# The first steps of a masked attention layer begin with one mask quarter and half of the heads; the other mask pieces and projections are made beside the steps

## The chip, the cores and the metric

The kernel runs on one core of a Trainium2 chip. Its time is device microseconds (us) of one execution, and the number that stands for a kernel is the median of several runs. Five engines work side by side: PE (TensorE, matrix products and transposes), DVE (VectorE), ACT (ScalarE), POOL (GpSimd) and SP (SyncE, which here only issues transfers). PEld is PE's loading of weights. Each engine runs its own queue in order and waits on semaphores for the others.

## The reference, cut to what matters

```python
# x: (8, 2048, 256) f32;  adj: (2048, 2048) int32, about 0.8% ones, symmetric, diagonal set
qkv = einsum('fnc,ck->fnk', x, w_qkv)             # H = 8 heads of D = 32
scores = einsum('fnhd,fmhd->fhnm', q, k) / sqrt(D)
scores = where(adj > 0, scores, -1e9)             # one mask for all entries and heads
t = einsum('fhnm,fmhd->fnhd', softmax(scores), v)
x1 = layernorm(x + t) * ln1_g + ln1_b
h = relu(x1 @ w1 + b1)
x2 = layernorm(x1 + h @ w2 + b2) * ln2_g + ln2_b
out = layernorm(x + x2)
```

## The kernel before

**Steps.** The main loop goes over `items`: 8 batch entries f, 4 quarters qc of 512 query rows, 2 groups g of 4 heads, 16 blocks mb of 128 keys. That is 1024 steps, 128 to an entry and 16 to a group. One step t does, in this order:

- `advance(t)`: some side work (below);
- `exponentials(items[t + 1])`: ACT, 128x2048, in place (L237);
- `scores(items[t + 2])` (`LEAD` is 2): PE makes the scores of four heads, transposed, keys in partitions (8 matmul records a step, L230), into two of three PSUM pairs; DVE adds the mask and writes the `p` tile, two instructions of 128x1024 (L233);
- `values(items[t])`: PE multiplies by the values (L249);
- `add_up(items[t])`: the sums over blocks. Of 16 blocks, six are added by POOL (L271) and six by transfers that POOL issues and that add in memory (L268); the block's tile is free after that. Four tiles (blocks 0, 1, 2 and 14) stay until the group's `denominator` has multiplied them by ones on PE (L315).

`p` tiles come from the pool `pp` with 12 buffers.

**The mask.** DVE adds it as float8: 0 where `adj` is set, -57344 elsewhere (int8 -5 has the same bits). A quarter has 8 pieces of 128x2x512 bytes, in the pool `mkp` of 9 buffers. All pieces also lie in device memory (`MD`), and `load_mask` (L151, on SP) fetches the next quarter's pieces in the second half of each quarter, one every second step, from step 17 of 32 on: 13 steps ahead of their first use.

**Side work.** Turned inputs (`turn`), queries (`ask`), keys and values (`project`) of the next entry, denominators, the division, the feed-forward part and the norms are generators in `fill`, sorted by a due step. `advance` gives PE a credit of 2200 a step; one product over 512 columns (in four column parts) costs 2048. A generator that yields `BANK` wants one of the PSUM banks for side work: at most one is started in a step, and only with a credit of 1024 or more left or something overdue; one that yields `MORE` holds its bank and goes on, in the next step if the credit is gone.

**The start.** `begin()` (L550 to L597) runs before step 0 and works through 16 chunks of `adj`, 512x512 each, quarter by quarter, fetched a little ahead into `p` tiles. For each, DVE compares the integers with 0 (L575, two instructions, bf16 out), PE turns the blocks (L141, 16 transposes), ACT casts one half to int8 (L147) and DVE takes the minimum with 1 into float8 for the other (L145); SP stores both in `MD`. With the chunks of quarter 0 go the turned inputs of entry 0, its first queries, and keys and values of the first head group (g = 0); with those of quarter 1, keys and values of g = 1. The scores of steps 0 and 1 come after quarter 1, and then the chunks of quarters 2 and 3.

Of the kernel before, what the change touches and what calls it, by code (L numbers as in the profile page):

```python
# [29 lines left out]
BANK, MORE, WAIT, TURNED, ROOM, INPUTS = -1, -2, -3, -4, -5, -10  # L30
STEP, UNIT, TURN, KEPT = 2200, 1024, 1400, 2200

MASKED = -57344.0
CODE = -5.0


# [25 lines left out]
def fast_path(ctx, tc, cst, x, adj, out, RS):  # L62
# [52 lines left out]
    def take(shape, dt):  # L115
        live.pop(0)
        live.append(ld.tile(shape, dt, name="in"))
        return live[-1]

    def give(t):  # L120
        live[:] = [None if u is t else u for u in live]


    MD = dp.tile([NCK, MB // 2, P, 2 * CH // 4], I32, name="md")
    MK = {}

    def words(mask):
        return mask.rearrange("p b q -> p (b q)").bitcast(I32)

    def mask_piece(t, qc, k):  # L130
        MK[t, qc, k] = mkp.tile([P, 2, CH], F8, name="mask")
        return MK[t, qc, k]

    def mask_blocks(qc, mc, cv, to=None):
        for half in range(2):
            yield BANK
            ps = bank(BF16)
            for r in range(2):
                for j in range(TPC):
                    rr = 2 * half + r  # L140
                    nc.tensor.transpose(ps[:, r, j * P:(j + 1) * P], cv[:, j, rr * P:(rr + 1) * P], identb)  # L141
            k = 2 * mc + half
            m = to[half] if to else mask_piece(0, qc, k)
            if half:
                nc.vector.tensor_tensor(m, ps, cst["ones"][:, 0:1, None].to_broadcast([P, 2, CH]), ALU.min, saturate=False)  # L145
            else:
                nc.scalar.copy(m.bitcast(I8), ps)  # L147
            nc.sync.dma_start(MD[qc, k], words(m))

    def load_mask(f, qc, k):  # L150
        nc.sync.dma_start(words(mask_piece(f, qc, k)), MD[qc, k])  # L151
# [5 lines left out]
    def queries(f, c, xT):  # L157
        for g in range(2):
            yield from channels(QT, qp, "qT", (f, c, g), xT, g * P)

    def turn_rows(xc, xT):
        for a in range(2):
            yield BANK
            ps = bank()
            transposes(ps, [xc[:, j, a * P:(a + 1) * P] for j in range(TPC)])
            nc.scalar.copy(xT[:, a, :], ps)
# [367 lines left out]
                resume(e, t)  # L534

    items = [(f, qc, g, mb) for f in range(F) for qc in range(NCK) for g in range(2) for mb in range(MB)]
    LEAD = 2
    FRAME = 2 * NCK * MB


# [7 lines left out]
            104: [(project, 0, 1)], 108: [(project, 1, 1)], 112: [(project, 2, 1)], 116: [(project, 3, 1)]}  # L548

    def begin():  # L550
        todo = deque((qc, c) for qc in range(NCK) for c in range(NCK))
        rows, cols = [], deque()

        def fetch():
            if todo:
                qc, c = todo.popleft()
                t = pp.tile([P, 4, CH], F32, name="p").bitcast(I32)
                nc.sync.dma_start(t, adj[qc * CH:(qc + 1) * CH, c * CH:(c + 1) * CH].rearrange("(j p) m -> p j m", p=P))
                cols.append((qc, c, t))

        for c in range(NCK):
            rows.append(pp.tile([P, 4, CH], F32, name="p"))
            xc = rows[c][:, 0:2, :].rearrange("p a (b c) -> p (a b) c", c=C)
            nc.sync.dma_start(xc, x[0, c * CH:(c + 1) * CH, :].rearrange("(j p) c -> p j c", p=P))
            fetch()
        fetch()
        while cols:
            qc, c, col = cols.popleft()
            if c % 2 == 0:
                two = pp.tile([P, 4, CH], F32, name="p").rearrange("p a q -> p (a q)").bitcast(BF16)  # L570
            cv = two[:, c % 2 * TPC * CH:(c % 2 + 1) * TPC * CH].rearrange("p (j m) -> p j m", m=CH)

            for half, what in enumerate((CODE, MASKED)):
                part = slice(half * 2 * P, (half + 1) * 2 * P)
                nc.vector.tensor_scalar(cv[:, :, part], col[:, :, part], 0.0, what, op0=ALU.is_le, op1=ALU.mult)  # L575
            fetch()
            xT = rows[c][:, 2:4, :]
            if qc == 0:
                yield from turn_rows(rows[c][:, 0:2, :].rearrange("p a (b c) -> p (a b) c", c=C), xT)
                nc.sync.dma_start(XD[0][c], xT)  # L580
                XT[0, c] = xT
                if c == 0:
                    yield from queries(0, 0, xT)
                yield from project(0, c, 0, xT)
            elif qc == 1:
                yield from project(0, c, 1, xT)
            if qc and c % 2 == 0:
                out4 = take([P, 4, 2, CH], F8)
                give(out4)
            yield from mask_blocks(qc, c, cv, [out4[:, c % 2 * 2 + i] for i in range(2)] if qc else None)  # L590
            if (qc, c) == (1, NCK - 1):
                for k in range(LEAD):
                    scores(items[k])
                exponentials(items[0])

    for _ in begin():
        pass  # L597
    state["side"] = 0
    for t, (f, qc, g, mb) in enumerate(items):
        if g == 1 and mb % 2 and (f + 1 < F or qc + 1 < NCK):  # L600
            load_mask(f + (qc + 1) // NCK, (qc + 1) % NCK, mb // 2)
        for what, *which in NEXT.get(t % FRAME, []):
            to = f if what is ask and which[0] else f + 1
            if to < F:
# [266 lines left out]
```

## Time and profile before

| | us |
|---|---|
| median of 5 runs | 3243.46 (3241.08 to 3250.44) |
| profiled execution, its own time | 3251.11 |
| its span, first to last instruction | 3249.2 |
| PE busy | 3114.1 (96%) |
| DVE busy | 2736.7 (84%) |
| ACT busy | 2437.0 (75%) |
| POOL busy | 2592.1 (80%) |
| first scores (L230) begin | 60.62 |
| third scores begin (the loop) | 98.34 |
| DMA engines, transfers that add (`p<-p`) | 66.9% of 16 engines' span |

How to read it: a line of the profile names the line of the code, the engine, the operation and `out<-in` by the program's tile names. In the timeline the first two numbers are the start and the length in us, and the bracket gives how long the engine idled before and what ended that. The granted clock (PEclk) is the share of full speed that TensorE was given. Busy time of PE holds pipelined matmuls, so 96% is not 96% of its peak. A queue name ending in q, as SPq, is an engine's issuing of a transfer; the time to landing is counted from there.

### The profile page before, as it was taken

To read this page: it belongs to the slowest core of one execution; us is meant where nothing else is said; L and a number is where in the kernel's file an instruction comes from. 1 tells how busy PE (TensorE), PEld (TensorE's weight loads), DVE (VectorE), ACT (ScalarE), POOL (GpSimd) and SP (SyncE) were. 2 spreads that over 40 slices of the span, in tenths; PEclk is the share of its full clock that TensorE was granted. 3 is DMA by queue.
4 is the path that set the end of the run, shared out by engine and by line. 5 is a ranking of instruction groups with operands and counts; after the bars stand their busy time and mean duration, and the time that the engine had idled before them with its cause. 6 is when DMAs were issued, how large, how long until landed. Compare 5 with 4: busy or idle time off the path is not lost.

```text
span 3249.2 us, 68406 instructions
## 1 busy us (share of the span) xinstructions
PE 3114.1 (96%) x28996; PEld 980.6 (30%) x28996; DVE 2736.7 (84%) x3203; ACT 2437.0 (75%) x1941; POOL 2592.1 (80%) x1358
## 2 busy tenths in 40 slices
PE   7899999999999999999999999999999999998985
PEld 4222333223332233322333323323233323332222
DVE  4788888888888888888988888888888888888975
ACT  3667778778777777778777778777778777777764
POOL 0578888888888888788887888888888788878884
PEclk8899999999999999999999999999999999999998
DMA  9688789778879788789788879878789778877763
GB/s 317 144 184 180 184 179 196 177 180 192 183 176 206 170 189 195 158 194 201 178 180 174 181 175 220 176 168 197 173 194 199 175 171 199 180 171 161 166 143 86
DMA packets 153240, 590.52 MB, mean 182 GB/s; under 512 B 15040, under 2 KB 67776, under 8 KB 103904
## 3 DMA queue, kind: packets, MB, share of 16 engines
q0 software_dynamic: 64416, 434.80, 66.9%
q1 hardware_dynamic: 87696, 149.98, 13.1%
q8 instruction: 229, 3.75, 0.4%
q10 hardware_dynamic: 816, 1.31, 0.1%
q14 instruction: 83, 0.68, 0.1%
HBM read 146.67 MB, written 37.75 MB: 57 GB/s over the span
## 4 chain that ended last, share of the span: by engine, by line
PE 75%; DVE 7%; POOL 5%; DMA 4%; issue 4%; ACT 2%; DVEq 0%; ACTq 0%; POOLq 0%
PE s L230 28%; PE x L249 24%; PE x L54 14%; PE x L315 6%; DVE p L233 5%; PE x L95 4%; DMA p<-p 3%; POOL p L271 2%; ACT p L237 1%; DMA mask<-md 1%; POOL y L365 1%; POOL y L363 0%; DVE st L278 0%; DMA y<-in_x_dram 0%; POOL y L461 0%
## 5 line engine op out<-in xcount | busy, mean ns | idle before, releaser
L233 DVE TENSOR_TENSOR p<-s,mask 128x1024 f32<-128x1024 f32 x2048 | 2410.8, 1219 | 375.1 <-PE s L230 214.4
L237 ACT ACTIVATE p<-p 128x2048 f32<-128x2048 f32 x1024 | 1956.9, 1911 | 523.2 <-DVE p L233 464.4
L271 POOL TENSOR_TENSOR p<-p 128x2048 f32<-128x2048 f32 x381 | 1823.6, 4788 | 227.5 <-ACT p L237 224.9
L230 PE MATMUL s<-qT,kT 32*128 32x512 f32 x8192 | 1175.4, 643 | 41.1 <-DVE p L233 36.2
L249 PE MATMUL x<-p,v 128*32 128x512 f32 x8192 | 1095.7, 607 | 17.2 <-ACT p L237 16.8
L268 POOL DMA_DIRECT2D p<-p x383 | 359.4, 957 | 307.0 <-ACT p L237 94.7
L230 PEld LDWEIGHTS s<-qT,kT 32*128 32x128 f32 x8192 | 321.4, 183 | 647.1 <-DVE p L233 587.6
L249 PEld LDWEIGHTS x<-p,v 128*32 128x32 f32 x8192 | 161.5, 108 | 799.6 <-issue 310.4
L315 PE MATMUL x<-p,ones 128*32 128x512 f32 x2080 | 270.0, 598 | 17.6 <-POOL p L271 11.1
L290 ACT ACTIVATE y<-y,nb,rs 128x256 f32<-128x256 f32 x372 | 219.1, 591 | 39.3 <-POOL nb L287 39.3
L54 PE MATMUL x<-in,wqkv 128*32 128x512 f32 x1888 | 243.5, 592 | 0.0
L278 DVE BATCH_NORM_STATS2 st<-y 128x6 f32<-128x256 f32 x372 | 155.4, 418 | 5.4 <-DMA y<-in_x_dram 5.4
L54 PE MATMUL x<-w2s,hT 128*32 128x256 f32 x2016 | 122.5, 384 | 1.7 <-DVE y L483 1.7
L54 PE MATMUL x<-turned,w1s 128*32 128x512 f32 x992 | 123.9, 598 | 0.0
L54 PEld LDWEIGHTS x<-wqkv,in 128*32 128x32 f32 x3584 | 102.2, 110 | 63.5 <-issue 59.0
L315 PEld LDWEIGHTS x<-p,ones 128*32 128x32 f32 x2080 | 66.3, 110 | 178.1 <-issue 140.7
L54 PE MATMUL x<-wqkv,in 128*32 128x128 f32 x3584 | 117.2, 273 | 0.0
L54 PEld LDWEIGHTS x<-in,wqkv 128*32 128x32 f32 x1888 | 61.7, 110 | 140.9 <-issue 113.7
L284 POOL TENSOR_TENSOR rs<-rs,mhalf 128x4 f32<-128x4 f32 x93 | 96.3, 1036 | 7.8
L54 PEld LDWEIGHTS x<-w2s,hT 128*32 128x32 f32 x2016 | 65.7, 111 | 74.8 <-issue 34.1
L363 POOL TENSOR_TENSOR y<-y,g2r 128x1024 f32<-128x1024 f32 x31 | 82.5, 2661 | 5.2 <-ACT y L290 5.2
L461 POOL TENSOR_TENSOR y<-y,be1b2r 128x1024 f32<-128x1024 f32 x31 | 83.0, 2679 | 0.6
(116 smaller groups left out, 1338.3 us busy)
## 6 DMA issues: line engine op xcount, KB each, us to landing
p<-p POOLq DMA_DIRECT2D x383, 1024.0 KB, 10.5
in<-xd SPq DMA_DIRECT2D x87, 512.0 KB, 10.6
mask<-md SPq DMA_DIRECT2D x248, 128.0 KB, 7.9
y<-in_x_dram POOLq DMA_DIRECT2D x62, 512.0 KB, 8.2
p<-in_adj_dram SPq DMA_DIRECT2D x16, 1024.0 KB, 9.7
out_dram<-y SPq DMA_DIRECT2D x31, 512.0 KB, 6.2
in<-in_x_dram SPq DMA_DIRECT2D x29, 512.0 KB, 15.9
xd<-in SPq DMA_DIRECT2D x28, 512.0 KB, 11.1
```

The source lines that it names most:

```text
L54: nc.tensor.matmul(out[r:r + D], lhsT[:, r:r + D], rhs, start=start, stop=stop)
L95: nc.tensor.transpose(ps[:, j * P:(j + 1) * P], s, ident)
L230: nc.tensor.matmul(ps2[half][:, j, :], KT[f, mb // TPC, g][r:r + D, (mb % TPC) * P:(mb % TPC + 1) * P], QT[f, qc, g][r:r + D, :], start=Tr ...
L233: nc.vector.tensor_tensor(pt[:, 2 * half:2 * half + 2, :], ps, MK[f, qc, mb // 2][:, mb % 2, None, :].to_broadcast([P, 2, CH]), ALU.add)
L237: nc.scalar.activation(PT[item], PT[item], AF.Exp, scale=1.0 / math.sqrt(D))
L249: nc.tensor.matmul(O[grp][r:r + D, :], V[f, mb // TPC, g][:, mb % TPC, r:r + D], PT[item][:, h, :], start=(mb == 0), stop=(mb == LAST))
L268: nc.gpsimd.dma_start(PT[f, qc, g, chain[0]], PT.pop(item), accum_op=ALU.add)
L271: nc.gpsimd.tensor_tensor(first, first, PT.pop(item), ALU.add)
L278: nc.vector.bn_stats(st, t[:, j, :])
L284: nc.gpsimd.tensor_tensor(rs, rs, cst["mhalf"], ALU.pow)
L290: nc.scalar.activation(t[:, j, :], t[:, j, :], AF.Identity, bias=nb[:, j:j + 1], scale=rs[:, j:j + 1])
L315: nc.tensor.matmul(ps[r:r + D, :], cst["ones"], term[:, h, :], start=(n == 0), stop=(n == len(blocks) - 1))
```

## The change

`begin()` now works on quarter 0 alone: four chunks of `adj`, turned inputs, the queries and the keys and values of g = 0, and both halves of each mask chunk cast by ACT. The turned inputs stay in four tiles that the feed-forward part uses later (two `y`, `turned`, `hT`). Then come the scores of steps 0 and 1 and the loop. The queries, keys and values of g = 1 are side work (`other_half`), due 3 steps ahead of their first scores.

The other 12 chunks are side work too (`mask_quarter`): those of quarter 1 start at steps 1, 6, 11, 16, those of quarter 2 at 32, 40, 48, 56, those of quarter 3 at 64, 72, 80, 88. Each takes one `p` tile, loads it by two transfers (512 rows of 256 integers each, 1 KB a row, where a row was 2 KB), waits seven steps, lets ACT cast the integers to bf16 in place (one half in a step, the other in the next), and then in two steps PE turns one half, DVE compares it out of PSUM straight to int8, and SP stores it in `MD`.

`load_mask` comes six steps later everywhere (`LATE`): from step 23 of 32 on, seven steps ahead of the first use; if a piece isn't made yet, side work is run until it is.

```diff
+    MK, MADE = {}, set()
+    def turn_mask(ps, cv):
+        state["credit"] -= 2 * TURN
+        for r in range(2):
+            for j in range(TPC):
+                nc.tensor.transpose(ps[:, r, j * P:(j + 1) * P], cv[j][:, r * P:(r + 1) * P], identb)
+    def convert(cv, col):
+        nc.vector.tensor_scalar(cv, col, 0.0, CODE, op0=ALU.is_le, op1=ALU.mult)
+    def mask_quarter(qc, c):
+        t = pp.tile([P, 4, CH], F32, name="p").rearrange("p a q -> p (a q)")
...
+        for h, part in enumerate(parts):
+            col = part.bitcast(I32).rearrange("p (j m) -> p j m", j=TPC)
+            nc.sync.dma_start(col, adj[qc * CH:(qc + 1) * CH, (2 * c + h) * 2 * P:(2 * c + h + 1) * 2 * P]...)
+        yield 7
+        for part in parts:
+            cv = part.bitcast(BF16).rearrange("p (a b m) -> p a b m", a=2, b=4)[:, :, 0:2, :]
+            cvs.append([cv[:, j // 2, j % 2] for j in range(TPC)])
+            nc.scalar.copy(cv, part.bitcast(I32).rearrange("p (a b m) -> p a b m", a=2, b=2))
+            yield 1
+        for h, part in enumerate(parts):
             yield BANK
             ps = bank(BF16)
...
+            turn_mask(ps, cvs[h])
+            m = part[:, half // 4:half // 2].bitcast(F8).rearrange("p (b q) -> p b q", b=2)
+            convert(m.bitcast(I8), ps)
+            nc.sync.dma_start(MD[qc, 2 * c + h], words(m))
+            MADE.add((qc, 2 * c + h))
...
-    LEAD = 2
+    LEAD, LATE = 2, 6
...
     def begin():
...
+        kept = [yp.tile([P, 2, CH], F32, name="y"), yp.tile([P, 2, CH], F32, name="y"),
+                work.tile([P, 2, CH], F32, name="turned"), work.tile([P, 2, CH], F32, name="hT")]
+        for c, xT in enumerate(kept):
...
+            for half in range(2):
+                part = slice(half * 2 * P, (half + 1) * 2 * P)
+                convert(cv[:, :, part], cols[c][:, :, part])
+            yield from turn_rows(rows[c], xT)
+            nc.sync.dma_start(XD[0][c], xT)
+            XT[0, c] = xT
+            if c == 0:
+                yield from channels(QT, qp, "qT", (0, 0, 0), xT, 0)
+            yield from project(0, c, 0, xT)
+            for half in range(2):
+                ps = bank(BF16)
+                turn_mask(ps, [cv[:, j, half * 2 * P:(half + 1) * 2 * P] for j in range(TPC)])
+                m = mask_piece(0, 0, 2 * c + half)
+                nc.scalar.copy(m.bitcast(I8), ps)
+                nc.sync.dma_start(MD[0, 2 * c + half], words(m))
+                MADE.add((0, 2 * c + half))
+        for k in range(LEAD):
+            scores(items[k])
+        exponentials(items[0])
+        for c in range(NCK):
+            start(0, other_half(c, kept[c]), MB + TPC * c - LEAD - 1)
+    def other_half(c, xT):
+        if c == 0:
+            yield from channels(QT, qp, "qT", (0, 0, 1), xT, P)
+        yield from project(0, c, 1, xT)
...
     for t, (f, qc, g, mb) in enumerate(items):
-        if g == 1 and mb % 2 and (f + 1 < F or qc + 1 < NCK):
-            load_mask(f + (qc + 1) // NCK, (qc + 1) % NCK, mb // 2)
+        uf, uqc, ug, umb = items[max(t - LATE, 0)]
+        if ug == 1 and umb % 2 and (uf + 1 < F or uqc + 1 < NCK):
+            while ((uqc + 1) % NCK, umb // 2) not in MADE:
+                advance(t, finish=True)
+            load_mask(uf + (uqc + 1) // NCK, (uqc + 1) % NCK, umb // 2)
+        if f == 0 and qc + 1 < NCK:
+            for c in range(NCK):
+                if t % (2 * MB) == (1 + 5 * c if qc == 0 else 8 * c):
+                    start(t, mask_quarter(qc + 1, c), 2 * MB * qc + MB + LATE - 2 + TPC * c)
```

More of the change, by code (lines that the diff above doesn't have):

```diff
@@ L31 @@
 STEP, UNIT, TURN, KEPT = 2200, 1024, 1400, 2200
-MASKED = -57344.0
 CODE = -5.0
@@ L124, in fast_path @@
     MD = dp.tile([NCK, MB // 2, P, 2 * CH // 4], I32, name="md")
-    MK = {}
+    MK, MADE = {}, set()
     def words(mask):
@@ L132, in mask_piece @@
         return MK[t, qc, k]
-    def mask_blocks(qc, mc, cv, to=None):
-        for half in range(2):
+    def turn_mask(ps, cv):
[7 more added lines that the diff above has]
+        t = pp.tile([P, 4, CH], F32, name="p").rearrange("p a q -> p (a q)")
+        half = TPC * CH // 2
+        parts = [t[:, h * half:(h + 1) * half] for h in range(2)]
+        cvs = []
+        for h, part in enumerate(parts):
+            col = part.bitcast(I32).rearrange("p (j m) -> p j m", j=TPC)
+            nc.sync.dma_start(col, adj[qc * CH:(qc + 1) * CH, (2 * c + h) * 2 * P:(2 * c + h + 1) * 2 * P].rearrange("(j p) m -> p j m", p=P))
+        yield 7
[5 more added lines that the diff above has]
+        for h, part in enumerate(parts):
             yield BANK
             ps = bank(BF16)
[L138 to L148, printed above, removed]
+            turn_mask(ps, cvs[h])
[3 more added lines that the diff above has]
+            MADE.add((qc, 2 * c + h))
     def load_mask(f, qc, k):
@@ L550, in begin @@
     def begin():
[L551 to L559, printed above, removed]
-        for c in range(NCK):
[L562 to L568, printed above, removed]
+        rows, cols = [], []
+        for c in range(NCK):
+            rows.append(pp.tile([P, 4, CH], F32, name="p")[:, 0:2, :].rearrange("p a (b c) -> p (a b) c", c=C))
+            nc.sync.dma_start(rows[c], x[0, c * CH:(c + 1) * CH, :].rearrange("(j p) c -> p j c", p=P))
+            cols.append(pp.tile([P, 4, CH], F32, name="p").bitcast(I32))
+            nc.sync.dma_start(cols[c], adj[0:CH, c * CH:(c + 1) * CH].rearrange("(j p) m -> p j m", p=P))
+        kept = [yp.tile([P, 2, CH], F32, name="y"), yp.tile([P, 2, CH], F32, name="y"),
+                work.tile([P, 2, CH], F32, name="turned"), work.tile([P, 2, CH], F32, name="hT")]
+        for c, xT in enumerate(kept):
             if c % 2 == 0:
@@ L571, in begin @@
             cv = two[:, c % 2 * TPC * CH:(c % 2 + 1) * TPC * CH].rearrange("p (j m) -> p j m", m=CH)
-            for half, what in enumerate((CODE, MASKED)):
+            for half in range(2):
                 part = slice(half * 2 * P, (half + 1) * 2 * P)
[L575 to L594, printed above, removed]
+                convert(cv[:, :, part], cols[c][:, :, part])
[21 more added lines that the diff above has]
+        yield from project(0, c, 1, xT)
     for _ in begin():
```

## The prediction

> **What bounds the kernel now.** I read the profile page first, then windows cut by stage, then the timeline of the start and the chain that ended last. The page's engine line and the costliest groups:
>
> ```profile
> PE 3114.1 (96%) x28996; PEld 980.6 (30%) x28996; DVE 2736.7 (84%) x3203; ACT 2437.0 (75%) x1941; POOL 2592.1 (80%) x1358
> ...
> L233 DVE TENSOR_TENSOR p<-s,mask 128x1024 f32<-128x1024 f32 x2048 | 2410.8, 1219 | 375.1 <-PE s L230 214.4
> ```
>
> PE is the bound of the average, DVE is not far behind. But the change touches the start and the first eighth, so the windows by stage matter more: everything ahead of the first scores (to 60.6), the rest of the preparation (to 98.3), the first 32 steps (two windows), the other 96 steps of the first batch entry, and one whole later entry.
>
> ```profile
> 0.00:60.60 60.60, 47.71 (x832) 30.95 (x832) 19.82 (x25) 23.79 (x35) 6.78 (x19) 0.97 0.99 337
> 60.60:98.30 37.70, 18.32 (x144) 13.82 (x144) 24.13 (x28) 11.09 (x10) 0.00 (x0) 0.53 0.51 178
> 98.30:141.20 42.90, 39.80 (x292) 9.74 (x294) 35.34 (x30) 29.64 (x19) 26.55 (x11) 0.94 0.74 169
> 141.20:183.80 42.60, 39.06 (x308) 10.04 (x308) 37.97 (x35) 32.66 (x21) 30.14 (x13) 1.00 0.84 186
> 183.80:470.30 286.50, 280.68 (x2536) 84.51 (x2533) 247.07 (x276) 220.93 (x168) 231.32 (x114) 0.99 0.82 182
> 855.10:1244.30 389.20, 383.87 (x3589) 119.53 (x3584) 336.67 (x392) 302.12 (x242) 326.76 (x170) 1.00 0.83 185
> ```
>
> Columns: window, length, busy us of PE, PEld, DVE, ACT, POOL, granted clock, DMA share, GB/s. From 60.6 to 98.3 PE works half the time at half its clock (0.53) and POOL does nothing: this is preparation with no main work beside it. The first entry takes 42.9 + 42.6 + 286.5 = 372.0 us with PE busy 359.5, a later one 389.2 with 383.9 (98.6%). DMA is at 0.74 to 0.84 throughout.
>
> The timeline shows what fills 60.6 to 98.3: one mask chunk after the other, each a comparison of the loaded integers (two halves), 16 transposes, one cast by ACT and one minimum by DVE, 3.8 us from one chunk's first comparison (86.73) to the next one's (90.54).
>
> ```profile
> 53.63 1.07 PE L141 MATMUL s<-identb,p 128*128 128x128 bf16 x16
> ...
> 60.62 1.14 PE L230 MATMUL s<-qT,kT 32*128 32x512 f32 x8 [1.32 <-DVE in L145]
> ...
> 86.73 1.29 DVE L575 TENSOR_SCALAR p<-p 128x1024 bf16<-128x1024 int32 x2
> ...
> 88.54 1.01 ACT L147 CAST in<-s 128x1024 int8<-128x1024 bf16 x1 [2.80 <-PE s L141]
> 89.40 1.23 DVE L145 TENSOR_TENSOR in<-x,ones 128x1024 fp8e5<-128x1024 bf16 x1 [1.38 <-PE x L141]
> ...
> 100.50 2.35 DVE L233 TENSOR_TENSOR p<-s,mask 128x1024 f32<-128x1024 f32 x2 [2.21 <-PE s L230]
> ```
>
> The chain of waits shows the two kinds of step: without side work DVE and scores alternate (105.43 to 107.92, 2.49 us); with one unit of side work PE has no gap (118.54 to 121.47, 2.93 us).
>
> ```profile
> 105.43 1.18 PE s L230 x8
> 106.64 1.24 DVE p L233
> 107.92 1.18 PE s L230 x8
> ...
> 118.54 1.07 PE s L230 x8
> 119.61 1.00 PE x L249 x8
> 120.61 0.86 PE x L54 x8
> 121.47 1.07 PE s L230 x8
> ```
>
> **What the start loses.** In the timeline the transposes of the last chunk of quarter 0 end at 40.90 (40.29 and 0.61 long), the first scores begin at 60.62. Between lie the four chunks of quarter 1 with the projections of heads 4 to 7, 4.6 us each; they go, 19.7 us. Against that, both pieces of a chunk of quarter 0 are now copied by ACT (1.01 each) where DVE had every second one; the copies of the next chunk's turned input queue behind, and that chunk's projections wait for those: 1.0 us at three chunk boundaries, 3.0 us. The first 1.7 us of queries saved in chunk 0 bring nothing, since DVE waits there for the adjacency (idle to 20.21). From the first scores to the adding of the third (60.62 to 100.50) pass 39.9 us; without the eight chunks it is the adding of steps 0 and 1, which took to 67.6, 7.0 us. Saved: 32.9. Together 19.7 - 3.0 + 32.9 = 49.6, say **50 us** (49 to 51; the row shows the first scores at half clock, and I leave them so).
>
> **What the first entry gains.** Moved in: projections of heads 4 to 7, four chunks of 3.6 us (45.43 to 49.03, the mask left out) and two units of queries, 0.86 each: 16.1 us of PE. 24 mask pieces of 8 transposes at 0.53 (half of the row of 16, 1.07): 12.8 us. So PE's 359.5 become 388.4; at the 98.6% of a later entry that takes 394 us, **+22** on 372.0. DVE alone would have room: 320.4 + 24 x 1.22 = 349.7.
>
> But the order inside a step costs more. A step starts at most one bank user, so a step with a mask piece has no unit. Its comparison stands on DVE ahead of the next adding (2.36): 1.22 + 2.36 against PE's 2.60. The adding of that step's scores waits for the comparison, the scores after them for its first half. The two pieces of a chunk come in successive steps; with a unit step behind them three steps take, by DVE, 1.22 + 2.36 twice, then 1.24 of the third adding and 1.14 of scores: 9.55, where PE has 2.60 + 2.60 + 2.93 = 8.13. Loss 1.4 x 12 chunks = 17. Part of it I take as hidden in gaps already in the 98.6% and in steps forced to double up: 13, **+35** in all (22 to 39).
>
> The comparison's price is not in the trace in this form (bf16 from PSUM to int8 with a constant). The nearest rows are L145, same source and width, 1.22, and L575, same operation but out of SBUF, 0.65. I take 1.22, for the source is PSUM. If it is 0.65, three steps take 8.4 and the loss is 3. The Trainium skill, "VectorE: DVE Perf Modes", section "The perf-mode tier table", says that an operation with a constant may run at two elements a cycle out of PSUM while one on two tensors may not, and L145 has two tensors. By that rule my estimate is half of 1.22, 0.61 us, and the sum would end 10 us lower; no run here shows it.
>
> ACT: 24 casts of 128x1024 out of SBUF at about 1.01 (the row of the PSUM cast; half of the 1.91 exponential is 0.96) and nine copies of 0.59. In a unit step ACT idles 1.02 (2.93 - 1.91), so a cast hides, if its data is there. They are in place, queued on ACT ahead of the next exponential: data late by L stops exponentials, then values. There is about 1.4 us of slack (from scores to values two steps, 5.86, less 2.4 and 1.91).
>
> SP: 24 loads of 512 KB in 1 KB rows, 24 stores of 128 KB, now behind and ahead of turned inputs and mask loads. SP is in order; a load whose p tile is not yet free holds up the mask loads behind it. POOL issues nothing new. P tiles: 12, of which heads and the steps in work hold 6 to 8; two or three mask tiles leave 2 to 3 spare where there were 4 to 6. One stall exists already at such a place: PE waits at L315 for a moved sum, 4.0 us (197.13), with DVE idle 6.57. I keep it, and put **+5** (0 to 25) for more of its kind at the group ends of steps 16 to 96.
>
> Masks for later quarters are loaded six steps later in all entries, seven steps ahead of use, 21 us; the page's median landing is 7.9, the longest of the tile's loads 24.8. I take 0 (0 to 15). The 98.6% hides it; without that cover each late piece costs its lateness.
>
> Sum for the profiled execution: 3249.2 - 50 + 35 + 5 = 3239.2 span. Its span is 5.7 above the median of the runs (3243.46; its own time 3251.11), so **3233**.
>
> **Rivals.** (1) *Adjacency late, slower.* The copy of a chunk's second half is eight steps, some 24.4 us, behind its load. Loads of 512 KB in 1 KB rows took 15.9 (in<-in_x) where 4 KB rows took 10.6, with the sums' transfers on the same engines:
>
> ```profile
> in<-xd SPq DMA_DIRECT2D x87, 512.0 KB, 10.6
> ...
> in<-in_x_dram SPq DMA_DIRECT2D x29, 512.0 KB, 15.9
> ```
>
> Two in a row could take 31.8: 7.4 late, less 1.4, is 6.0 per chunk; the first two chunks are loaded before the sums start, so up to 10 x 6 = 60, 3293; half of them, 3263. It decides from two late chunks on (12 us against the forecast's 10). For it: DMA is at 0.74 to 0.84, and 12.6 MB more at the 397 GB/s that the window 40 to 50 us shows are 32 us of all engines in some 300, a tenth. Against: SP runs ahead of the others, and DMA has holes. The skill's "DMA: Bandwidth & Descriptors", section "Queues, rings and completion order", has the engines alternate between queues packet by packet, which speaks against the change: by my estimate each 1 KB row would wait behind an 8 KB one of the sums, and lateness would be the rule; the 15.9 here is milder.
>
> (2) *Cheaper than thought.* The comparison at 0.65 or the pairs spread over steps; the loss of 13 and the 5 go: -50 + 22 = -28, 3215. For: DVE has 22 us to spare even then. Against: adding and scores alternate strictly.
>
> (3) *The later mask loads bite in every entry*: if in each of some 30 quarters one piece is late by 1 us, +30, 3263. Against: median 7.9 in 21.
>
> **How the numbers follow.** Forecast 3233, 0.52, its own range 3217 to 3246; rival 1 0.28, rival 2 0.15, rival 3 0.05. Range: 3212 (rival 2 and a little) to 3263 (rival 1 at half). The measurement tells 0.2%, 6.5 us, from no change. Faster: 0.36 of the forecast, all of rival 2, 0.01 of rival 1: 0.52. Same: 0.12 and 0.02: 0.14. Slower: the rest, 0.34.
>
> **What would show it.** First scores near 44 us, third adding near 51, no half-clock stretch of 40 us; first entry 407 to 415 us long; the comparison's row near 1.22; DVE alternating comparison and adding in pairs of steps at 3.6 us. Wrong if ACT's idle before the new casts is put down to the adjacency (rival 1), if DVE waits for p tiles, or if entries 2 to 8 change by over 1 us each (rival 3).

## The result: slightly slower, by 0.14%

The kernel after takes 3247.85 us (median of 30 runs) against 3243.62 for the kernel before (50 runs): ratio 1.0014, 95% interval 1.0009 to 1.0019. The forecast was 3233, faster. The profiled execution of after takes 3250.83 us, its span is 3249.1, against 3251.11 and 3249.2. Two equal spans: what the start won is gone again. This section shows where, stage by stage.

**The start went as the forecast has it.** The timeline of after (start, length, engine, line, operation; in brackets the idle time before and its cause):

```profile
42.67 1.93 ACT L591 CAST mask<-x 128x1024 int8<-128x1024 bf16 x2
43.01 1.14 PE L245 MATMUL s<-qT,kT 32*128 32x512 f32 x8
44.28 4.84 DVE L248 TENSOR_TENSOR p<-s,mask 128x1024 f32<-128x1024 f32 x4 [10.94 <-ACT mask L591]
...
49.31 2.36 DVE L248 TENSOR_TENSOR p<-s,mask 128x1024 f32<-128x1024 f32 x2 [0.19 <-issue]
```

First scores at 43.01 (forecast 44), the third adding at 49.31 where it was at 100.50: 51.2 us won.

**The first entry then loses them.** Taking the start of the same step's exponential in both traces (single executions, that of before 7.5 us above its median and that of after 3.0), after stands against before at -47.9 us in step 16, -37.1 in step 48, -27.4 in 64, -19.0 in 80, -10.3 in 96, -5.2 in 128, +3.0 in 144, +9.9 in 224 and 256, and then comes down again: +6.6 in 528, +4.6 in 784, +0.1 in 1023. So from the loop's start (-51.2) the first 128 steps cost 46 more than before (forecast 40), the next hundred another 15, and the rest gives 10 back. The 15 are side work that was pushed over the end of the first entry: PE is busy for 390.7 us in the second one, where it was for 380.3. The windows of after, from the loop's start on (window, length, busy us of PE, PEld, DVE, ACT, POOL, granted clock, DMA share, GB/s):

```profile
49.00:110.00 61.00, 57.71 (x624) 18.78 (x624) 48.90 (x43) 47.66 (x35) 35.69 (x13) 1.00 0.75 181
110.00:198.00 88.00, 80.23 (x688) 24.54 (x684) 74.40 (x73) 60.53 (x42) 58.00 (x24) 0.98 0.86 199
198.00:312.00 114.00, 102.72 (x828) 31.28 (x824) 92.17 (x100) 81.35 (x64) 78.12 (x38) 0.94 0.81 193
312.00:387.00 75.00, 67.19 (x609) 21.97 (x610) 61.52 (x70) 53.52 (x44) 51.97 (x27) 0.95 0.76 176
387.00:465.00 78.00, 77.76 (x672) 23.27 (x675) 69.72 (x84) 62.83 (x52) 64.13 (x38) 1.00 0.94 216
```

Until 387, while chunks of the mask are in work, PE idles 9 to 10% in three windows, and the granted clock falls to 0.94. After 387 it is full again (77.76 of 78). DVE, for its part, is never above 0.89. The groups of lines in 49 to 465 name what DVE waited for, and give the two new operations:

```profile
L248 DVE TENSOR_TENSOR p<-s,mask 128x1024 f32<-128x1024 f32 x255 | 300.2, 1219 | 63.5 <-PE s L245 31.0 <-DMA md<-p 10.6 <-DMA p<-p 6.8
...
L140 DVE TENSOR_SCALAR p<-x 128x1024 int8<-128x1024 bf16 x24 | 29.3, 1219 | 2.9 <-PE x L137 2.9
L154 ACT CAST p<-p 128x1024 bf16<-128x1024 int32 x24 | 24.9, 1037 | 0.0
```

`md<-p` is the store of a mask piece, `p<-p` a transfer that adds sums. An adding that waits for one of them waits for its `p` tile: these 17.4 us are the first sign of what the forecast made small. The casts of ACT (1.04 each) never waited for the adjacency (0.0), and its loads came fast:

```profile
p<-in_adj_dram SPq DMA_DIRECT2D x24, 512.0 KB, 7.4
```

The chain of waits of after between 150 and 320 has such stores on it: it follows the adding at 205.34 back to a store issued 23 us before, for which DVE itself idled 3.80 us.

```profile
181.13 1.14 DVE p L140
182.29 22.97 DMA md<-p
205.34 1.24 DVE p L248
...
269.30 1.23 DVE p L140
270.55 6.38 DMA md<-p
277.12 1.24 DVE p L248
...
302.59 13.40 DMA p<-p
316.11 1.24 DVE p L248
```

By the trace, the 12 chunks hold their `p` tile from the issue of the load to the last store for 31 to 73 us each, some 600 us together: at 340 us from the first load (45.0) to the last store (384.2) that is 1.75 of the 12 tiles. The chunks wait for the bank, which side work with an earlier due step takes first.

### The profile page after: what moved, and what is told of

Same layout as the page of the kernel before. It is cut to its first block, busy times and chain, and to the rows that moved or that the text cites. A ratio compares the mean times of both kernels' runs of the same rounds, so it can differ in the third digit from the quotient of the medians.

```text
span 3249.1 us, 68445 instructions
## 1 busy us (share of the span) xinstructions
PE 3111.7 (96%) x28996; PEld 977.9 (30%) x28996; DVE 2730.9 (84%) x3187; ACT 2448.8 (75%) x1957; POOL 2591.1 (80%) x1358
## 4 chain that ended last, share of the span: by engine, by line
PE 78%; DVE 6%; POOL 4%; issue 4%; DMA 3%; ACT 1%; DVEq 0%; ACTq 0%; POOLq 0%
PE s L245 28%; PE x L264 25%; PE x L53 15%; PE x L330 6%; DVE p L248 4%; PE x L94 4%; POOL p L286 2%; DMA p<-p 1%; DMA md<-p 1%; ACT p L252 1%; POOL y L380 1%; POOL y L378 1%; DVE p L140 0%; DVE st L293 0%; DMA y<-in_x_dram 0%
## 5 line engine op out<-in xcount | busy, mean ns | idle before, releaser
L248 DVE TENSOR_TENSOR p<-s,mask 128x1024 f32<-128x1024 f32 x2048 | 2410.9, 1219 | 408.4 <-PE s L245 229.8
L264 PE MATMUL x<-p,v 128*32 128x512 f32 x8192 | 1097.2, 608 | 15.6 <-ACT p L252 15.2
L53 PE MATMUL x<-turned,w1s 128*32 128x512 f32 (+1 forms) x1024 | 126.0, 593 | 2.6 <-ACT hT L432 2.0
L380 POOL TENSOR_TENSOR y<-y,be2r 128x1024 f32<-128x1024 f32 x31 | 83.3, 2687 | 0.2
## 6 DMA issues: line engine op xcount, KB each, us to landing
in<-in_x_dram SPq DMA_DIRECT2D x29, 512.0 KB, 10.6
```

Source lines behind the costliest of these rows:

```text
L53: nc.tensor.matmul(out[r:r + D], lhsT[:, r:r + D], rhs, start=start, stop=stop)
L248: nc.vector.tensor_tensor(pt[:, 2 * half:2 * half + 2, :], ps, MK[f, qc, mb // 2][:, mb % 2, None, :].to_broadcast([P, 2, CH]), ALU.add)
L264: nc.tensor.matmul(O[grp][r:r + D, :], V[f, mb // TPC, g][:, mb % TPC, r:r + D], PT[item][:, h, :], start=(mb == 0), stop=(mb == LAST))
L380: nc.gpsimd.tensor_tensor(z, z, rows(cst["be2r"]), ALU.add)
```

## The experiments

Ratios are to the kernel before on the same chip, in five rounds. Where a part is worth so many us, that is the ratio's difference times 3243.46; a ratio's interval is 0.0008 to 0.0017 to each side (0.0005 for after), so a difference of two has some 4 to 7 us of uncertainty. Kernels marked * leave part of the mask out: their later quarters use the pieces of quarter 0.

**1. Without the masks of quarters 1 to 3 (*).**

```diff
-                    start(t, mask_quarter(qc + 1, c), 2 * MB * qc + MB + LATE - 2 + TPC * c)
-        nc.sync.dma_start(words(mask_piece(f, qc, k)), MD[qc, k])
+        nc.sync.dma_start(words(mask_piece(f, qc, k)), MD[0, k])
```

> After, but the masks of quarters 1 to 3 are not made at all (the steps of those quarters add quarter 0's mask instead, loaded at the same places). It leaves the start and the projections of heads 4 to 7 beside the steps, so it prices the twelve mask chunks alone. Saved at the start 51 us, projections 16 us of PE: if those fill PE at its usual share, 3243.6 - 51 + 16 = 3209, that is 39 us below after (3247.9): 13 of transposes, 26 of comparisons' order and waits. If instead the projections or the later mask loads eat the gain, it stays within 15 us of after.

Measured 3200.44 us, ratio 0.987 (0.9853 to 0.9887): -42.2. After stands at +4.5. The masks made in the steps therefore cost 46.7 us, where the forecast's 40 for the first entry has 24 for them and 16 for the projections.

**2. A tile of its own for the compared piece.** So no store holds a `p` tile.

```diff
-            m = part[:, half // 4:half // 2].bitcast(F8).rearrange("p (b q) -> p b q", b=2)
+            m = mp.tile([P, 2, CH], F8, name="m")      # pool mp, 2 buffers; pool mkp 9 -> 8
```

> After, but the compared mask piece goes into a small tile of its own (2 buffers of 1 KB, mkp 8 buffers instead of 9), so that the p tile is free once the second half is transposed and not only when the stores have landed. Theory A (p tiles held too long): DVE's waits for md<-p (10.6 us in after) and part of the half-clock windows (23.9 us in the first 390, half of it lost) go: 8 to 15 us faster than after, 3233 to 3240. Theory B (the comparison's place on DVE costs all): within 3 us of after.

Measured 3236.55, ratio 0.9989 (0.998 to 0.9998): 8 us better than after. The waits for stores are worth about that, not more.

**3. The comparison by ACT, in its cast** (scale 5, bias -5; the piece is then copied out of the bank by ACT, and DVE has nothing to do with the later masks).

```diff
-            nc.scalar.copy(cv, part.bitcast(I32)...)
+            nc.scalar.activation(cv, part.bitcast(I32)..., AF.Identity, bias=cst["code"], scale=-CODE)
-            convert(m.bitcast(I8), ps)
+            nc.scalar.copy(m.bitcast(I8), ps)
```

> After, but ACT makes -5 or 0 in the first cast (scale and bias) and casts the transposed piece out of PSUM to int8, so the 24 comparisons leave DVE and 24 casts of about 1.01 come to ACT. Theory B (comparison ahead of the adding, 1.4 us per pair of pieces): 12 to 17 us faster than after, 3231 to 3236. Theory A: the waits for p tiles stay, 0 to 5 faster; slower, if ACT's two more casts delay the exponentials.

Measured 3247.28, ratio 1.002 (1.001 to 1.0031): no gain, though 29.3 us of work left DVE. The waits of its DVE between 45 and 450 (engine and line, what it waited for: us, times, longest) show what took the place:

```profile
DVE p L249 <- DMA p<-p: 21.3, 7, 5.2
DVE p L249 <- DMA md<-p: 11.8, 2, 8.3
```

After has 17.4 us in these two rows, this kernel 33.1.

**4. The kernel before, with its mask loads six steps later, alone.**

```diff
-    LEAD = 2
+    LEAD, LATE = 2, 6
-        if g == 1 and mb % 2 and (f + 1 < F or qc + 1 < NCK):
+        uf, uqc, ug, umb = items[max(t - LATE, 0)]
+        if ug == 1 and umb % 2 and (uf + 1 < F or uqc + 1 < NCK):
```

> Before with one part of the change alone: the mask loads six steps later in all entries. Theory C (the later loads bite in every entry): 5 to 30 us slower than before. Theories A and B: within 3 us of before, 3243.6.

Measured 3234.07, ratio 0.9978 (0.9969 to 0.9986): this part of the change gains 7 us. By steps it stands at -1.9 us against before in step 208, -6.2 in 464, -12.1 in the last: a little in most entries. (These are single executions again, and the first 1.9 us are there before the first step, where the two kernels do the same.)

**5. Mask chunks due early** (ten steps after their start, ahead of other side work at the bank).

```diff
-                    start(t, mask_quarter(qc + 1, c), 2 * MB * qc + MB + LATE - 2 + TPC * c)
+                    start(t, mask_quarter(qc + 1, c), t + 10)
```

> After, but each mask chunk is due ten steps after its start, when its casts are done, so its two pieces go ahead of other side work; in after a chunk holds its p tile for 31 to 73 us from load to last store (595 us in all, 1.75 tiles on average over 340 us). Theory A (the p tiles that masks hold are the lost time): the holds fall to about 35 us each, some 430 in all, and the time by 4 to 10 us below after. Theory D (the work itself, in whatever order, costs what it costs): within 3 us of after.

Measured 3249.85, ratio 1.0019 (1.0009 to 1.0029): nothing gained. But the tiles were still held for some 541 us together, where 600 had been and 430 were expected, so this says little of what shorter holds are worth.

**6. The own tile, the casts four steps after the load in place of seven, due after seven steps.**

```diff
-        yield 7
+        yield 4
```

> The own tile for the compared piece (8 us faster than after), casts four steps after the load instead of seven (loads land in 7 to 9 us, casts waited for none), and due seven steps after the start: a chunk holds its p tile for some 8 steps, 25 us, 300 in all. Theory A: 14 to 22 us faster than after, 3226 to 3234, below the kernel with only the later mask loads (3234). Theory D: no better than the own tile alone, 3237.

Measured 3253.16, ratio 1.0034 (1.0021 to 1.0046), slower. Its waits between 49 and 465 show rival 1's mechanism, which after does not have:

```profile
ACT p L155 <- DMA p<-in_adj_dram: 18.3, 5, 7.8
...
PE x L265 <- ACT p L253: 16.4, 6, 8.0
```

Casts that come at four steps wait for the adjacency (18.3 us), exponentials behind them on ACT come late, and PE's values wait (16.4). Four steps are too few.

**7. The same with the comparison by ACT.** (Edits of 6 and 3 together.)

> The kernel before this one with the comparison made on ACT. With the comparison on DVE two pieces and a unit step take 9.55 us by DVE where PE has 8.13. If that loss is real and was only covered by waits for p tiles when the comparison was moved in after, it shows here: 8 to 15 us faster than the kernel before this one. If the order on DVE costs nothing at all: within 3 us; slower if ACT's 24 more casts reach the exponentials.

Measured 3259.3, ratio 1.0058 (1.0043 to 1.0074): no gain again. It fits that ACT now has more to do ahead of the exponentials; that was not tested alone.

**8. The kernel before with 10 `p` tiles in place of 12.**

```diff
-    pp = ctx.enter_context(tc.tile_pool(name="pp", bufs=12))
+    pp = ctx.enter_context(tc.tile_pool(name="pp", bufs=10))
```

> Before with 10 p buffers instead of 12, in all 1024 steps. It prices the p tiles alone: the masks of after hold 1.75 of them over some 112 steps. Theory A: 112 steps of 1024 lose some 15 us, so the whole loses 60 to 140 us, 3300 to 3380. Theory D: p tiles are in plenty, within 10 us of before.

Measured 3407.26, ratio 1.0507 (1.0493 to 1.0521). Two tiles fewer for the whole kernel cost 163 us, 5%, more than theory A had: the supply of tiles has nothing to spare. 1.75 tiles for 340 us, at this rate, are 15 us (0.0507 x 340 x 1.75 / 2).

The next two runs take the masks in the steps apart into two halves.

**9. Only the tiles (*).** Tile taken, adjacency loaded and cast, two stores; the bank turns are taken in the schedule, but no transposes and no comparison are issued.

```diff
-            ps = bank(BF16)
-            turn_mask(ps, cvs[h])
+            state["credit"] -= 2 * TURN
             m = part[:, half // 4:half // 2].bitcast(F8)...
-            convert(m.bitcast(I8), ps)
```

> The kernel after, with each step-quarter's p tile taken, loaded, cast by ScalarE and held until two stores of a slice of it are done, at the same steps as in the change, but without the bank, the 16 transposes and the two comparisons of a chunk; later steps load the first quarter's mask pieces, as in the run without quarters 1 to 3, which is the run to compare with (ratio 0.987, some 42 us below the kernel before). Theory A (the masks made in the steps cost more than forecast because their chunks hold p tiles, which are short): 20 us or more of the 46.7 come back, ratio 0.993 or above. Theory B (they cost more because the transposes, the bank and the comparison stand in the way of the steps' own work on TensorE and VectorE): at most 10 us come back, ratio 0.987 to 0.990.

Measured 3233.05, ratio 0.997 (0.996 to 0.9979): 32 us above experiment 1. Theory A's side. DVE waits 24.3 us for tiles that a transfer still holds (15.6 for `p<-p`, 8.7 for `md<-p`, between 45 and 450), in experiment 1 for none. The stores here wait for no bank, so the tiles are held for some 420 us together, not for 600 as in after.

**10. Only the work (*).** Bank, transposes (of the identity), comparison into an own tile, store; no `p` tile, no load, no cast.

```diff
-        t = pp.tile([P, 4, CH], F32, name="p")...   # and its loads and casts
+        yield 7; yield 1; yield 1
...
+            turn_mask(ps, None)                      # identb in place of cv
+            m = mp.tile([P, 2, CH], F8, name="m")
             convert(m.bitcast(I8), ps)
```

> The other half of it: per piece the bank, eight transposes (of the identity matrix), the comparison by VectorE into a tile of its own, and the store, at the same steps; no p tile, no load of the adjacency and no cast, and later steps load the first quarter's mask pieces. To compare with the run without quarters 1 to 3 (ratio 0.987). Theory A (p tiles): 13 to 17 us come back, the 12.8 us of transposes with little on top, ratio 0.991 to 0.9922. Theory B (work on TensorE, VectorE and the bank): 30 us or more come back, ratio 0.9963 or above.

Measured 3225.7, ratio 0.9944 (0.993 to 0.9957): 24 us above experiment 1, between the theories. 32 and 24 make 56 of 46.7: the halves overlap, and neither is as small as forecast.

**11. Own tile and comparison by ACT.** (Edits of 2 and 3 together.)

> The kernel after, with the comparison done by ScalarE in its cast (scale 5, bias -5, two values a piece in place of a test), the piece then copied by ScalarE from the bank into a tile of its own, so that VectorE does nothing for the later masks and no store holds a p tile. 24 comparisons of 1.22 us leave VectorE. Theory A: beside the run with the own tile alone (ratio 0.9989) nothing is gained, 0.998 to 1.000. Theory B, where VectorE's order is what costs: the 13 us that the forecast put on it come off, ratio 0.994 to 0.996.

Measured 3244.78, ratio 1.0006 (0.9995 to 1.0016), against 0.9989 with the own tile alone: not better, rather 5 us worse. The waits of its DVE name the adding transfers:

```profile
DVE p L250 <- DMA p<-p: 18.4, 7, 3.6
```

In experiment 2 the same row has 7.7 us. With tiles held, time freed on DVE is spent waiting for the next tile.

**12. The kernel before, with later mask loads, and one value for quarters 2 and 3**, so that ACT copies both halves of those chunks out of PSUM and DVE's minimum (L145) goes.

```diff
-            for half, what in enumerate((CODE, MASKED)):
+            for half, what in enumerate((CODE, MASKED if qc < 2 else CODE)):
...
-            if half:
+            if half and qc < 2:
```

> The kernel before with mask loads 6 steps later (which alone gave 0.9978), and in quarters 2 and 3 of the mask, made ahead of the steps, both halves of a piece hold the small code and are copied out of PSUM by ScalarE, so that VectorE, which carries that stretch, loses eight evictions. If VectorE's chain sets that stretch's pace, 1.7 us a chunk come off in eight chunks: some 14 us, ratio 0.993 to 0.995. If the half clock of TensorE sets it, or the loads of the adjacency, nothing beyond 0.9978.

Measured 3219.57, ratio 0.9932 (0.9918 to 0.9945): 22 us below the kernel before, the best of the kernels that make the whole mask. 7 of it are the later loads, 15 the start (expected 14): its third scores begin at 84.38, where before has 98.34. Its window from the first scores on (clock 0.71) holds 12 us of the loop; up to 84.4 the clock is 0.67, where before had 0.53 up to its loop:

```profile
60.60:96.00 35.40, 24.57 (x208) 12.92 (x200) 22.67 (x27) 23.57 (x21) 1.68 (x1) 0.71 0.61 207
```

The next four cut the two halves further.

**13. Only the tiles, without the casts (*).**

```diff
-            nc.scalar.copy(cv, part.bitcast(I32)...)
```

> The run that only holds the tiles (ratio 0.997), less the 24 casts of 1.04 us by ScalarE: tiles taken, loaded, held to the same step and stored. If the tiles and their transfers carry its 32 us: 0.995 to 0.997. If the 25 us that the casts take of ScalarE carry it: 0.989 to 0.991.

Measured 3236.84, ratio 0.9985 (0.9977 to 0.9994): nothing comes back (37 us above experiment 1). The casts' 25 us on ACT do not carry the cost.

**14. Only the tiles, stored earlier (*).** The two stores right after the casts, the bank turns after that.

```diff
         for h, part in enumerate(parts):
-            yield BANK
-            state["credit"] -= 2 * TURN
             m = part[:, half // 4:half // 2].bitcast(F8)...
             nc.sync.dma_start(MD[qc, 2 * c + h], words(m))
+        for h in range(2):
+            yield BANK
+            state["credit"] -= 2 * TURN
```

> The run that only holds the tiles (ratio 0.997), with the two stores of a chunk issued right after its casts instead of after its turns at the bank, which are still taken in the same order: a tile is held for some 9 steps, not for 10 to 24. If the time that tiles are held is what costs, half or more of the 32 us goes: 0.990 to 0.992. If the loads, casts and stores cost it, whenever the tile comes free: 0.995 to 0.997.

Measured 3227.96, ratio 0.9956 (0.9944 to 0.9968): 5 us come back, which is within the uncertainty. But the edit hardly shortened the holds: from the issue of the load to that of the last store the 12 tiles are held for some 406 us together, in experiment 9 for some 420. What the time in hand is worth, this run does not tell.

**15. Only the work, without the comparison (*).**

```diff
-            convert(m.bitcast(I8), ps)
-            m = mp.tile([P, 2, CH], F8, name="m")
+            m = blank                                # a constant tile
```

> The run that only does the work (ratio 0.9944, 25 us above the run without quarters 1 to 3), less the 24 comparisons of 1.22 us on VectorE; the bank, the transposes and a store of a constant tile stay. If the 12.8 us of transposes are all that stays: 0.991 to 0.992, and VectorE's 29 us were worth the other 12. If the bank's turns and the transposes alone carry it: 0.9935 to 0.9945.

Measured 3201.17, ratio 0.9873 (0.9858 to 0.9889): 1 us above experiment 1, less than either theory had. Over the whole kernel the transposes, the bank turns and the stores cost nothing that can be told from zero, with some 7 us of uncertainty; the comparison costs 23. By steps, this kernel is 8 us behind experiment 1 in step 128 and 14 in step 144, and level with it from step 592 on. So where they stand they do cost something (a table behind experiment 18 has the sums); why later entries give the lag back was not tested.

**16. No `p` tile for quarters 2 and 3.** Their chunks as halves of 4 KB a partition in the buffers for turned inputs; own tile for quarter 1.

```diff
+    def mask_half(qc, k):
+        yield INPUTS - 1
+        t = take([P, TPC, C], F32)                   # one of three, given back after the store
...
+                if qc and t % (2 * MB) == 4 * k:
+                    start(t, mask_half(qc + 1, k), 2 * MB * qc + MB + LATE - 2 + 2 * k)
```

> The kernel after, with the stores of quarter 1 out of a tile of their own, and the chunks of quarters 2 and 3 as halves of 4 KB a partition in the three buffers that the inputs of later frames use, each asked for when one is free: 16 of the 24 pieces take no p tile. Nothing of the computation changes. If held p tiles are what the forecast missed: 0.993 to 0.9965, 10 to 20 us below the kernel after. If it is the work that the pieces bring, the run with the own tile alone is not bettered: 0.998 to 1.000.

Measured 3263.82, ratio 1.0073 (1.0061 to 1.0086): both theories missed, it is 19 us slower than after. The waits for adding transfers did go (DVE waits 2.7 us for `p<-p` between 45 and 450), but the waits of DVE for scores grew from 30.4 to 49.7:

```profile
DVE p L268 <- PE s L265: 49.7, 50, 6.9
...
DVE p L268 <- DMA p<-p: 2.7, 1, 2.7
```

The pieces now queue for three buffers with the next entry's inputs. Which of the delays that follow costs the 19 us was not settled, so a gain from freed tiles beyond the 8 us of experiment 2 is not shown in a kernel with the whole computation.

**17. Only the work, with a copy by ACT in place of the comparison by DVE (*).**

```diff
-            convert(m.bitcast(I8), ps)
+            nc.scalar.copy(m.bitcast(I8), ps)
```

> The run that only does the work (ratio 0.9944), with the 24 comparisons out of PSUM by VectorE replaced by 24 copies by ScalarE; without any reader of the bank it was 0.9873. If VectorE's time is what the comparison costs: 0.987 to 0.9895. If it is the bank held until some engine has read it, or if ScalarE has no more room than VectorE: 0.993 to 0.9955.

Measured 3211.43, ratio 0.9906 (0.9891 to 0.992), between the two expectations: 11 us above no reader, 12 below the comparison on DVE. So of the comparison's 23, about half is there because it is DVE that does it. The other half can be the bank, held until some engine has emptied it, or the 24 copies on ACT's own queue; the run does not part the two.

The windows from 45 to 450 of the runs without tiles, in the order of experiments 1, 15, 17 and 10 (columns as above, busy us of PE, PEld, DVE, ACT, POOL):

```profile
45.00:450.00 405.00, 399.44 (x3668) 121.27 (x3672) 352.71 (x380) 313.35 (x231) 318.86 (x151) 1.00 0.80 176
```

```profile
45.00:450.00 405.00, 400.75 (x3728) 126.61 (x3728) 345.68 (x371) 305.90 (x224) 311.27 (x145) 1.00 0.80 180
```

```profile
45.00:450.00 405.00, 394.15 (x3644) 125.01 (x3648) 336.93 (x360) 319.23 (x244) 304.96 (x141) 0.99 0.78 175
```

```profile
45.00:450.00 405.00, 385.57 (x3496) 120.91 (x3492) 353.90 (x373) 292.71 (x216) 295.39 (x139) 0.99 0.78 174
```

Look at PE and DVE. In the first two kernels PE is 99% busy. The second has 192 transposes more to do, but within this window it has only 60 PE instructions more and 4 additions less (274 for 278): it is behind here, and level at the end. In the fourth DVE is as busy as in the first (353.9 and 352.7), but 29.2 of that are comparisons, its additions fall from 278 to 261 in the same 405 us, and PE falls to 95%. That fits a DVE with little room left in these steps, so that what it does for the masks is lost to the additions. It is a reading of rows, not a proof: the third kernel lies 11 us behind with DVE at 83%.

**18. Only the tiles, without casts, with a quarter of the bytes (*).** The same tiles held over the same steps, 128 KB loaded per half in place of 512.

```diff
-            nc.sync.dma_start(col, adj[qc * CH:(qc + 1) * CH, ...])
+            nc.sync.dma_start(part[:, half // 4:half // 2].bitcast(I32), MD[0, 2 * c + h])
```

> The run that holds the tiles without casts (ratio 0.9985), with 128 KB loaded per half chunk from the first quarter's pieces in place of 512 KB of the adjacency; tiles, steps and stores as there. If the held tiles cost the 35 us: 0.9965 to 0.9985. If the 9.4 MB less of transfers is what counts: 0.989 to 0.992.

Measured 3220.64, ratio 0.9927 (0.9911 to 0.9942): 19 us below experiment 13, still 18 above experiment 1. Both theories hold for a part each: by the medians about 18 us for holding the tile and 19 for the 9.4 MB more that are loaded, by the traces (table below) 22 and 10. What DVE waited for between 45 and 450 (us, times, longest) shows where it is lost, first experiment 13, then 18:

```profile
DVE p L245 <- DMA p<-p: 17.3, 10, 4.8
DVE p L245 <- DMA md<-p: 11.8, 2, 7.7
```

```profile
DVE p L245 <- DMA p<-p: 12.9, 7, 3.3
DVE p L245 <- DMA md<-p: 5.8, 1, 5.8
```

That is 29.1 us of waiting for a tile with the loads in full and 18.7 with a quarter of them; in experiment 1 there is no such row, and the kernels that hold no tile (10, 15, 17) have 3 us at most. So the cost of the tiles, and much of what the loads add, is DVE without a free `p` tile. Why the loads make it longer is open. The loads themselves land in time. The adding transfers, which have to land before their `p` tile is free, are no clear answer (KB each, median us to landing between 45 and 450; experiments 1, 13 and 18, then after):

```profile
p<-p POOLq DMA_DIRECT2D x52, 1024.0 KB, 10.0
```

```profile
p<-p POOLq DMA_DIRECT2D x48, 1024.0 KB, 11.4
...
p<-in_adj_dram SPq DMA_DIRECT2D x22, 512.0 KB, 7.8
```

```profile
p<-p POOLq DMA_DIRECT2D x48, 1024.0 KB, 10.7
```

```profile
p<-p POOLq DMA_DIRECT2D x46, 1024.0 KB, 10.4
```

Of these they are slowest beside the full loads of experiment 13, but 10.4 in after, which has these loads too, and 10.8 in experiment 15, which has none.

**The prices by stage.** The same traces, cut by the start of the exponentials of steps 2, 256 and 1023: the first two entries, where all the moved work stands, and the other six, where these kernels have the same work (us, one execution each).

| kernel | first two entries | above experiment 1 | the other six |
|---|---|---|---|
| before | 752.2 | -8.8 | 2344.0 |
| 1, no later masks | 761.0 | | 2342.2 |
| 15, work without comparison | 769.8 | +8.8 | 2331.8 |
| 17, with a copy by ACT | 779.3 | +18.3 | 2330.0 |
| 10, with the comparison by DVE | 788.7 | +27.7 | 2334.9 |
| 18, tiles with small loads | 783.3 | +22.3 | 2341.2 |
| 13, tiles without casts | 793.6 | +32.6 | 2343.9 |
| 9, tiles | 796.3 | +35.3 | 2335.9 |
| after | 813.3 | +52.3 | 2334.2 |

Experiment 15 is level with experiment 1 at the end only because its other six entries are 10 us shorter, for a reason that is not known (10, 15 and 17 also have a mask pool of 8 buffers in place of 9). So two readings stand for the transposes, the bank turns and the stores: 1 us by the medians, 9 by the first two entries. The turns at the bank are also part of the "tiles" in 9, 13, 14 and 18.

## Why the prediction was wrong

By its own steps, in us against the kernel before:

| step | forecast | the runs |
|---|---|---|
| start | -50 | -51.2 in the trace |
| projections of g = 1 moved in | +16 | +16.1 by difference (-42.2 of experiment 1 is -51.2 - 7.1 + 16.1); +8.8 in the traces' first two entries |
| later mask loads | 0 (0 to +15) | -7.1 (experiment 4) |
| masks in the steps | +24 | +46.7 (after less experiment 1) |
| sum | -10 | +4.5 |

- **The start** was right in both its parts: the first scores 17.6 us earlier (forecast 16.7), from there to the third adding 33.6 us less (32.9). The **projections** cost 9 to 16; they were never run alone.
- **The later mask loads** had the wrong sign: the forecast bounded them from below by nothing and never asked whether a gain was possible. Why there is one was not tested. Nothing of rival 3 is seen.
- **The masks in the steps** were mis-sized by 23 us, and this decided the sign. The term that failed is the one for `p` tiles, +5 (0 to 25). Tiles and loads alone cost 32 to 37 us (experiments 9 and 13), in two parts that the forecast had as 5 and as nothing: some 18 to 22 for the tile and 10 to 19 for the loads (experiment 18). The number of tiles in use was right ("two or three", 1.75 on average by the trace), not the price: the forecast had counted "2 to 3 spare" where experiment 8 shows that two are worth 5%. Its own sign, "if DVE waits for p tiles", came: 17.4 us in after, 24.3 and 29.1 in experiments 9 and 13, none in experiment 1. A chunk held its tile for up to 73 us in after; what shorter holds would be worth was not shown (experiments 5 and 14 hardly shortened them).
- **The end of the first entry** was taken as the end of the cost: 388.4 us of PE at 98.6% busy. The entry became 46 us longer (forecast 40), but PE, 93% busy there, ran only 288 of the some 520 instructions that moved in (3412 from 49.0 to 465.1, where before has 3124 from 98.3 to 470.3). The rest ran in the second entry (3744 against 3511) and made it 15 us longer, where the forecast had nothing.
- **The work of the pieces**, 12.8 for transposes and 13 for the order on DVE, measured 24 alone, near its 26; that is luck, for the parts differ. The transposes, with the bank's turns and the stores, cost 1 by the medians and 9 by the traces' first two entries, where 12.8 stood; the comparison costs 23 by the medians and 19 by the traces, where 13 stood. "DVE alone would have room" failed: most of the comparisons' 29 us came off the end.
- **Both together** cost less than their sum (46.7 for 56). It fits that the same DVE time is lost to one or the other: emptying the bank by ACT gains 12 without tiles held (experiments 10 and 17) and nothing with them (3 and 11). How a single stall is shared between them stays open.
- **The comparison's price**, 1.22 taken from L145, was right: 1.219. The Trainium skill, "VectorE: DVE Perf Modes", "The perf-mode tier table", allows an operation with a constant up to two elements a cycle out of PSUM, by which the forecast gave 0.61 as an estimate. The 24 comparisons, bf16 in PSUM to int8, took 1.219 each, and the measurement decides: no run here shows the faster rate with int8 out, and rival 2 falls with it. The pairs of steps looked as forecast, adding behind comparison (timeline of after):

```profile
115.16 1.14 PE L245 MATMUL s<-qT,kT 32*128 32x512 f32 x8
116.02 1.22 DVE L140 TENSOR_SCALAR p<-x 128x1024 int8<-128x1024 bf16 x1
117.15 2.35 DVE L248 TENSOR_TENSOR p<-s,mask 128x1024 f32<-128x1024 f32 x2
...
118.42 1.14 PE L245 MATMUL s<-qT,kT 32*128 32x512 f32 x8 [0.53 <-DVE p L248]
```

- **Rival 1** (adjacency late) did not happen with the change's seven steps: loads landed in 7.4 us (median), not in 15.9, and no cast waited. It is real at four steps (experiment 6). The skill's "DMA: Bandwidth & Descriptors", "Queues, rings and completion order", has engines alternate between queues by packets. The forecast's estimate from it, that each small row waits behind a large one and lateness is the rule, did not come true in after. Who pays instead, no run here shows: the loads took 7.4 in after and 11.4 in experiment 2, the adding transfers 10.4 in after and 10.8 in before.

## What to carry to other kernels

Before moving preparation into a main loop, price the buffers and transfers it borrows by a run of the kernel with fewer buffers; what is taken from a pool that is just large enough can cost more than the work that moves in. A busy share alone does not price more work: here 24 instructions more on the engine at 87% cost 19 to 23 of their 29 us, and 192 on the one at 99% cost 1 to 9 of their 12.8. And work that an entry cannot take does not vanish at its end: follow it into the next. And give a moved load a range on both sides of zero.

The better way here was to shorten the start where it stands: later mask loads and one engine less in its chain gave 3219.57 us (0.9932, 0.9918 to 0.9945), with nothing added to the loop.

## What the runs showed of the hardware that was not expected

- DVE compares 128x1024 bf16 out of PSUM to int8 in 1219 ns, as long as it adds two tensors of f32 at that size (1219).
- TensorE's granted clock was lower inside the loop where PE had gaps: 0.94 from 198 to 312 us of after, with PE 90% busy, and 1.00 from 387 to 465, with PE at 99.7%; from 45 to 450 it was 0.97 in after and 1.00 in experiment 1.
- How long 512 KB in rows of 1 KB take to land is not told by their size: the adjacency took 7.4 us (median) in after, with the engines 82% busy between 45 and 450, and 11.4 in experiment 2; the inputs (`in<-in_x_dram`) took 15.9 in the page of before and 10.6 in that of after. What makes the difference was not tested.
